# Layer 1's q and k of a head pair by seven products of quarters

## The chip, the cores and the metric

The kernel runs on one core of a Trainium2 chip. The metric is the device time of one launch in microseconds (us); the figure for a kernel is the median of its runs. Before the change it is 3814.2 us (three runs, 3813.44 to 3816.28). Everything is computed in 32-bit floats.

## The reference, cut to what matters

Two attention layers run one after the other on four images of 32 x 32 tokens with 768 channels, each behind a group norm and with a residual. Layer 1 is the one that changes:

```python
qkv = x @ w_qkv.T + b_qkv
q, k, v = (qkv[0], qkv[1], qkv[2])
q = layer_norm(dwconv3x3(q, w_pool_q), g_q, b_q)
k = layer_norm(dwconv3x3(k, w_pool_k), g_k, b_k)
v = layer_norm(dwconv3x3(v, w_pool_v), g_v, b_v)
attn = jnp.einsum('bqc,bkc->bqk', qf * scale, kf)
attn = attn + rel_h[:, :, :, :, None] + rel_w[:, :, :, None, :]   # after a reshape
o = softmax(attn) @ vf + q
x = x + o @ w_proj.T + b_proj
```

There are 12 heads of 64. The change touches only `x @ w_qkv.T` for q and k.

## The kernel before, in words

**Tiles.** The 1024 tokens of an image lie along the free axis in two halves of 512 (`HALF`), the 768 channels as six chunks of 128 partitions. Two heads make a **pair** (128 rows of q, k or v); a stage, which is one image in one layer, has six pairs. The stages run in the order (image 0, layer 0), (1, 0), (0, 1), (1, 1), then the same for images 2 and 3: 8 stages, 48 pairs, of which 24 are of layer 1.

**The clock of the program.** `attend(pair)` (L720) gives out 16 steps per pair. Steps 0, 4, 8 and 12 emit a block of four score tiles (L820 and L822, and four exponentials on ScalarE, L827); steps 2, 6, 10 and 14 emit the 16 matmuls of the weighted sum that eat them (L844). Between two `yield`s the main loop takes the pieces that `events` holds for that step. So, while pair A is attended, the pieces of the pairs behind it are emitted; TensorE, VectorE, ScalarE and GpSimd have a manual schedule, and the emission is the order of their queues. A pair's plan (L643) gives each piece a number r; the piece of pair i falls in step 16(i-1)+r. So r from 0 to 15 is "pair A+1 in step r of A", and r from -8 to -2 is "pair A+2 in step r+16 of A". SyncE, which issues the loads and stores of SBUF, is not in the manual schedule.

**A pair of layer 1, before the change.** q, k and v each take six chunk products per half: `padded` (L517) makes 12 calls of a 64-column matmul (`halves`, L128, L131) into one PSUM bank, and ScalarE then writes the half into a padded image with two instructions (L527). VectorE runs the nine taps of the convolution (`taps`, L531: L542 once, L544 eight times), centres (L559, L560), sums squares (L570, L571), normalises (L157 to L160, L582), and for v that last step writes `vt`, which the weighted sum reads. By steps of the attended pair A:

- pair A+1: step 2 and 4 v halves; 2 to 6 taps of k; 3 centre q; 6 and 7 squares and norm of q; 8 centre k; 8 to 11 taps of v; 9 transposes of q back (`back`, L586) and its copies; 10 and 11 positions, and squares of k; 12 norm of k and `split` (L624: L630 on VectorE, then 16 DMAs on GpSimd's queue that lay out the position bias); 13 centre v; 14 transposes of k back; 15 squares and norm of v.
- pair A+2: step 9 and 10 the two q halves (8 and 10 for some pairs), 12 and 14 the two k halves, 12 to 15 eight of the nine taps of q; the ninth comes in step 0 of the next pair.
- pair A itself: in steps 4 and 12 four VectorE instructions of `result` (L800 to L805); in steps 2 and 10 `restore_last`, which needs the one small PSUM bank.

**PSUM.** `bank()` hands out half-size banks from the two places b and c that the score tiles also use, in the order that `behind_scores` and `behind_av` give; the next user of a place waits until the last reader of its bank is done. `small_bank` is one bank of its own.

**Weights.** `uses` lists the weight loads in the order of their use; two buffers, and `used()` issues the load of the use after next.

**Quarters, as they exist before.** Layer 0 (pairs 2 and on, `sevens`, L391) and the projections (`project`, L858) already multiply a 2 x 2 arrangement of quarters by seven products instead of eight. There the weight sums are made once by `mix_weights` (L268) and kept in DRAM, and the token sums lie in SBUF (`mix_tokens`).

Of the kernel before, what the change touches and what calls it, by code (L numbers as in the profile page):

```python
# [17 lines left out]
P = 128  # L18
B = 4
S = 32  # L20
# [25 lines left out]
def two_layers(ctx: ExitStack, tc: tile.TileContext, keep, x_in, wqkv, wproj, rels, windows, vrow, small, const, onehot, picks, out):  # L46
# [122 lines left out]
    def rows(x):  # L169
# [6 lines left out]
    V_SUMS, PROJ_SUMS = NC, NC + NC // 2  # L176
    mixed = [
        dram.tile([P, N_SUMS, NC // 2, P], F32, tag=f"mixed{u}", name=f"mixed{u}")
        for u in range(PROJ_SUMS + 2 * (NC // 2))
    ]  # L180
    mixed_there = set()
# [14 lines left out]
    terms = [part(2 * T + 9 * HALF + i * HALF, HALF) for i in range(2)]  # L196
    counts = {"pad": 0, "y": 0, "c": 0, "v": 0}
# [5 lines left out]
    def in_sevens(i):  # L203

        return items[i][1] == 0 and i >= 2

# [11 lines left out]
    for i, (_, layer, hp) in enumerate(items):  # L218
        first = (i - 1) * 16 + shift(i)
        if in_sevens(i):  # L220
            uses += [(first, (i, 0, 0)), (first + 0.1, (i, 0, 1)), (first + 2, (i, 0, 2)), (first + 2.1, (i, 0, 3))]
            if hp % 2 == 0:
                uses += [(first + 8, (i, 2, 0)), (first + 8.1, (i, 2, 1)), (first + 10, (i, 2, 2)), (first + 10.1, (i, 2, 3))]
        else:
            uses += [(first + r, (i, s)) for s, r in enumerate((-8, -4, 2) if layer else (0, 4, 8))]
# [15 lines left out]
    def load_weights(n):  # L241

        if n >= len(uses):
            return
        i, s, *some = uses[n]
        _, layer, hp = items[i]
        w = wp.tile([P, NC, P], F32, tag="wqkv", name="wqkv_t")
        weights[uses[n]] = w
        if not some:
            nc.sync.dma_start(w, wqkv[layer, hp, :, s])  # L250
        elif some[0] == 0:
            (pa, sa), (pb, sb) = two(i, s)
            nc.sync.dma_start(w[:, :3, :], wqkv[0, pb, :, sb, 3:])
            nc.sync.dma_start(w[:, 3:, :], wqkv[0, pa, :, sa, :3])
        else:
            load_sums(w, hp if s == 0 else V_SUMS + hp // 2, some[0])
# [11 lines left out]
    def mix_weights(u):  # L268
# [4 lines left out]
        if u < PROJ_SUMS:  # L273
            (pa, sa), (pb, sb) = two(u, 0) if u < V_SUMS else two(2 * (u - V_SUMS), 2)
            nc.sync.dma_start(a, wqkv[0, pa, :, sa])
            nc.sync.dma_start(b, wqkv[0, pb, :, sb])
        else:
            layer, m = divmod(2 * (u - PROJ_SUMS), NC)
            for i, w in enumerate((a, b)):
                nc.sync.dma_start(w, wproj[layer, :, :, m + i, :].rearrange("h p q -> p h q"))  # L280
        yield
        a1, a2, b1, b2 = a[:, :3, :], a[:, 3:, :], b[:, :3, :], b[:, 3:, :]
        for n, to, x, y, op in (
# [11 lines left out]
    def mix_tokens(stage):  # L295
# [3 lines left out]
        for to, x, y, op in (  # L299
# [3 lines left out]
            nc.vector.tensor_tensor(to, x, y, op)  # L303
            yield
# [70 lines left out]
    class Pair:  # L375
# [11 lines left out]

        def make_vt(self):
            self.vt = work.tile([P, NKT, P], F32, tag="vt", name="vt")
# [111 lines left out]
        def put_k(self, ps, h, scale, bias):  # L501
            if self.k is None:
                self.k = work.tile([P, T], F32, tag="k", name="k")
# [13 lines left out]
        def padded(self, s, h):  # L517
# [3 lines left out]
            ps = self.product(s, h)  # L521
            ps = ps.rearrange("p (a c) -> p a c", a=S)

            for g, own, there in ((h, slice(0, S // 2), 1), (1 - h, slice(-1, None) if h == 0 else slice(0, 1), 0 if h == 0 else S // 2 + 1)):
# [4 lines left out]
                )  # L529

# [112 lines left out]
        def plan(self):  # L643
# [14 lines left out]
            if not self.layer:  # L658
# [18 lines left out]
            pieces = [  # L677
                (-8 if early_late else -7, lambda: self.padded(Q, 0)),
                (-6, lambda: self.padded(Q, 1)),
                (-4, lambda: self.padded(K, 0)),  # L680
                (-2, lambda: self.padded(K, 1)),
# [301 lines left out]
    def at(step, piece):  # L983
        events.setdefault(step, []).append(piece)
# [3 lines left out]
    for k in range(1, len(stages)):  # L988
# [3 lines left out]
        for r in range(12):  # L992
            at(first + 2 * n_steps + 2 + 3 * r, lambda norm=norm: next(norm, None))
# [11 lines left out]
    for u, call, step in (  # L1005
        (2, 0, 5), (7, 6, 11), (3, 13, 18), (4, 22, 29), (8, 31, 38), (5, 40, 47), (0, 49, 55), (6, 57, 63), (1, 65, 71),
        (9, 72, 77), (10, 78, 83), (11, 84, 89), (12, 124, 135), (13, 137, 147), (14, 149, 159),
# [358 lines left out]
```

## Time and profile before

The table is of the profiled execution, which took 3816.61 us by its own clock; its span, first to last instruction, is 3814.6 us. The median of the three timed runs is 3814.2.

| engine | busy us | share of the span |
|---|---|---|
| TensorE matmul (PE) | 3749.5 | 98% |
| VectorE (DVE) | 2467.1 | 65% |
| ScalarE (ACT) | 1786.5 | 47% |
| GpSimd (POOL) | 529.1 | 14% |

The granted TensorE clock is 0.997. DMA moved 330.44 MB, a mean of 87 GB/s. A pair of layer 0 takes some 55 to 75 us and a pair of layer 1 some 72 to 74 us between the first score matmuls of two attended pairs, longer where a projection runs beside it (up to 114 us). "PE busy" is pipelined matmul time, so the useful reading of it is how little is left idle. Idle time of another engine matters only where TensorE waits for it.

### The profile page before, as it was taken

The page shows a single profiled execution, that of the slowest core. Times are in us where ns is not written, and L with a number is a line of the kernel's source. Part 1 is how long each engine was busy: PE and PEld are TensorE (multiplying, and loading weights), DVE is VectorE, ACT ScalarE, POOL GpSimd, SP SyncE. Part 2 cuts the span into 40 slices and gives each one's busy share as a digit, 9 for nine tenths or more (in the row PEclk, how much of TensorE's full clock was granted, in tenths as well). Part 3 has the DMA queues.
Part 4 walks back from the last instruction along what each step waited for, and adds up shares of the span by engine and source line. Part 5 has one row for each costly group of instructions (what it writes and reads, how often), then busy time and mean ns, then how long its engine had stood idle before and what let it go on. Part 6 is the DMA issues. An engine that isn't in the chain of part 4 may idle for free. (4 is left out here: it accounts for less than half of the span.)

```text
span 3814.6 us, 76313 instructions
## 1 busy us (share of the span) xinstructions
PE 3749.5 (98%) x32990; PEld 1656.7 (43%) x32990; DVE 2467.1 (65%) x3068; ACT 1786.5 (47%) x2573; POOL 529.1 (14%) x964
## 2 busy tenths in 40 slices
PE   8999999999999999999999999999999999999998
PEld 4535535533344443444535445355343444434442
DVE  2566554559678877688454554445686888867874
ACT  2455434545355553455534544254442555525562
POOL 0111100111111211111200010001111112111120
PEclk9999999999999999999999999999999999999999
DMA  4344443331431223311333132523114212142123
GB/s 152 102 122 116 134 144 90 101 81 40 119 102 48 57 59 95 123 48 48 82 111 121 53 78 63 171 61 78 46 46 131 87 50 66 47 122 65 48 58 100
DMA packets 214024, 330.44 MB, mean 87 GB/s; under 512 B 50390, under 2 KB 103698, under 8 KB 213680
## 3 DMA queue, kind: packets, MB, share of 16 engines
q1 hardware_dynamic: 122912, 211.86, 17.9%
q0 software_dynamic: 90768, 113.61, 12.6%
q8 instruction: 263, 4.31, 0.5%
q14 instruction: 81, 0.66, 0.1%
HBM read 184.23 MB, written 40.10 MB: 59 GB/s over the span
## 5 line engine op out<-in xcount | busy, mean ns | idle before, releaser
L827 ACT ACTIVATE e<-s 128x1024 f32<-128x1024 f32 x768 | 775.6, 1024 | 423.7 <-PE s L822 393.6
L131 PE MATMUL qkv<-xn,wqkv_t 128*64 128x512 f32 x3648 | 816.0, 596 | 7.0 <-DVE gmean L334 2.6
L820 PE MATMUL s<-q,k 64*128 64x512 f32 x3072 | 808.7, 603 | 6.6 <-ACT e L827 3.1
L544 DVE SCALAR_TENSOR_TENSOR shared<-shared,sm 128x1056 f32<-128x1056 f32 x576 | 757.9, 1316 | 15.7
L822 PE MATMUL s<-bias,ones 64*128 64x512 f32 x1536 | 611.7, 790 | 1.1 <-DMA bias<-whole 1.0
L844 PE MATMUL av<-e,vt 128*64 128x512 f32 x2624 | 596.2, 596 | 0.0
L131 PEld LDWEIGHTS qkv<-xn,wqkv_t 128*64 128x64 f32 x3648 | 256.5, 137 | 484.0 <-issue 466.1
L640 POOL DMA_DIRECT2D bias<-high x384 | 205.6, 556 | 1794.6 <-ACT high L629 1559.7
L838 DVE TENSOR_TENSOR acc<-acc,e 128x1024 f32<-128x1024 f32 x294 | 360.0, 1225 | 114.0 <-ACT e L827 87.4
L820 PEld LDWEIGHTS s<-q,k 64*128 64x128 f32 x3072 | 279.5, 186 | 264.4 <-issue 213.3
L527 ACT ACTIVATE shared<-qkv,sm 128x512 f32<-128x512 f32 (+1 forms) x288 | 129.3, 502 | 469.7 <-PE qkv L131 469.7
L844 PEld LDWEIGHTS av<-e,vt 128*64 128x64 f32 x2624 | 185.4, 137 | 350.9 <-issue 316.8
L822 PEld LDWEIGHTS s<-bias,ones 64*128 64x128 f32 x1536 | 148.6, 187 | 185.4 <-issue 184.1
L640 POOL DMA_DIRECT2D bias<-whole x384 | 207.2, 571 | 53.2 <-DVE whole L630 46.3
L836 DVE TENSOR_TENSOR acc<-e 128x1024 f32<-128x1024 f32 x49 | 60.0, 1225 | 215.4 <-ACT e L827 206.8
L742 ACT COPY weighed<-av 128x512 f32<-128x512 f32 x96 | 56.3, 587 | 279.0 <-PE av L844 270.1
L559 DVE TENSOR_REDUCE mean<-ln_c 128x8 f32<-128x512 f32 x144 | 98.6, 685 | 106.0 <-PE ln_c L556 106.0
L771 POOL DMA_DIRECT2D weighed<-last x94 | 50.7, 541 | 679.6 <-ACT last L768 638.6
L613 PEld LDWEIGHTS rel<-q,rel 64*32 64x32 f32 x6144 | 112.1, 106 | 68.6 <-issue 63.8
L613 PE MATMUL rel<-q_t,rel 64*32 64x32 f32 x6144 | 123.6, 195 | 1.8 <-issue 1.8
L613 PE MATMUL rel<-q,rel 64*32 64x32 f32 x6144 | 122.7, 195 | 1.9 <-issue 1.9
L412 DVE TENSOR_TENSOR shared<-shared,m3m 128x512 f32<-128x512 f32 x66 | 45.3, 687 | 119.9 <-PE m3m L131 119.8
(162 smaller groups left out, 4439.0 us busy)
## 6 DMA issues: line engine op xcount, KB each, us to landing
bias<-high POOLq DMA_DIRECT2D x384, 128.0 KB, 2.9
bias<-whole POOLq DMA_DIRECT2D x384, 128.0 KB, 3.0
wqkv_t<-in_wqkv SPq DMA_DIRECT2D x78, 384.0 KB, 3.2
wqkv_t<-mixed SPq DMA_DIRECT2D x66, 384.0 KB, 3.1
wproj_t<-mixed SPq DMA_DIRECT2D x48, 384.0 KB, 3.3
wqkv_t<-in_wqkv SPq DMA_DIRECT2D x66, 192.0 KB, 2.5
xn<-in_x SPq DMA_DIRECT2D x24, 512.0 KB, 7.7
x<-in_x SPq DMA_DIRECT2D x48, 256.0 KB, 3.2
```

Source lines behind the costliest of these rows:

```text
L131: nc.tensor.matmul(ps[lo : lo + D], a[:, lo : lo + D], b, start=start, stop=stop, **kw)
L527: nc.scalar.activation(self.pad[s][:, rows, there : there + src.shape[2]], src, AF.Identity, bias=col(self.column(s)))
L544: nc.vector.scalar_tensor_tensor(y, window, tap, y, ALU.mult, ALU.add)
L559: nc.vector.tensor_reduce(of, heads, AX.X, ALU.add)
L613: nc.tensor.matmul(ps[lo : lo + S, k * S : (k + 1) * S].rearrange("p (b c) -> p b c", b=2), rel[rows, 2 * self.layer + i, first : first + ...
L640: nc.gpsimd.dma_start(sets, some.unsqueeze(1).to_broadcast([D // 2, 2, QC]))
L820: nc.tensor.matmul(ps[:, j, :], k[rows, keys], q[rows, cols], start=True, stop=False)
L822: nc.tensor.matmul(ps[:, j, :], ones[rows, kt % 2 * P : (kt % 2 + 1) * P], bias[c][rows, kt // 2, :], start=False, stop=True,)
L827: nc.scalar.activation(e, ps, AF.Exp)
L836: nc.vector.tensor_tensor(acc, es[0], es[1], ALU.add)
L838: nc.vector.tensor_tensor(acc, acc, e, ALU.add)
L844: nc.tensor.matmul(av[j * D : (j + 1) * D, :], pair.vt[:, kt, j * D : (j + 1) * D], e[:, j, :], start=(kt == 0), stop=(kt == NKT - 1),)
```

## The change

For 22 of the 24 pairs of layer 1 (all but the first pair after layer 0, twice), q and k of a pair are one product of a 2 x 2 arrangement: rows q and k, columns the two token halves, inner index the two groups of three channel chunks. It is done by seven products of three chunks each (`seven`, 6 matmul calls) in the form with few sums of results. Terms:

- `sum_tokens` makes four token sums per chunk column of a stage once, on VectorE (12 instructions of 128 x 512 per stage), and stores each in DRAM (`tokens`), in nine pieces from step 62 of the stage before. `call` loads one kind of sum (three blocks of 256 KB) from DRAM; each pair calls four kinds in turn into the same three blocks.
- `mix_weights` makes the weight sums of the six pairs once (24 VectorE instructions in all) while layer 0 runs, and stores them.
- `products(n)`: n=0 in step 6 of A (three products w1, w6, w2), n=1 put first in step 8 (w7), n=2 in step 9 (w4), n=3 in step 12 (w5), n=4 in step 14 (w3). They replace the four halves that stood in steps 9, 10, 12 and 14. One half still goes out through ScalarE (`put_from`); the three others by `put_padded` on VectorE (one instruction of 128 x 512 with a running sum, one copy of a column of 128 x 32). Three more VectorE additions of 128 x 512 make the running sums.
- The group norm of a layer-1 stage begins 7 steps earlier. `k` and `vt` change from two rotating buffers to named ones; layer 1 has one of each, and the spare ones hold the blocks and the running sums. The times of some weight mixes move.

The other pieces of the plan keep their steps. The diff, cut:

```diff
+    def in_products(i):
+
+        return items[i][1] == 1 and items[i - 1][1] == 1
...
+        elif in_products(i):
+            uses += [(first + r, (i, 0, n)) for n, r in enumerate((-10, -8, -7, -2))] + [(first + 2, (i, 2))]
...
+        if u >= LATE_SUMS:
+
+            t1, t2 = (
+                wp.tile([P, HALF], F32, tag="x", name="mix")[:, : 3 * P].rearrange("p (n c) -> p n c", c=P) for _ in range(2)
+            )
+            for n, to, x, y in ((3, t1, b1, a1), (0, t2, b2, t1), (1, b1, b2, b1), (2, a2, a2, t2)):
+                nc.vector.tensor_tensor(to, x, y, ALU.subtract)
+                nc.sync.dma_start(mixed[u][:, n], to)
...
+    def sum_tokens(stage):
+
+
+        for n in range(NC // 2):
+            x11, x12, x21, x22 = (xns[stage][:, n + k, h : h + HALF] for h in (0, HALF) for k in (0, 3))
+
+            def keep_sum(which, x, y, op):
+                to = wp.tile([P, HALF], F32, tag="x", name="token_sum")
+                nc.vector.tensor_tensor(to, x, y, op)
+                nc.sync.dma_start(tokens[stages.index(stage) % 2][which, n], to)
+                return to
...
         def make_vt(self):
-            self.vt = work.tile([P, NKT, P], F32, tag="vt", name="vt")
+            self.vt = one.tile([P, NKT, P], F32, tag=self.home("vt"), name="vt")
...
+        def call(self, which):
+
+
+            if which == S2:
+                two_blocks = one.tile([P, 2, HALF], F32, tag="vt0", name="blocks")
+                self.blocks = [two_blocks[:, 0], two_blocks[:, 1], third_block]
+            for n, block in enumerate(self.blocks):
+                nc.sync.dma_start(block, tokens[stages.index((self.b, self.layer)) % 2][which, n])
+
+        def seven(self, ps, at, x, more=False):
+
+            w = weights[self.i, 0, at // 2][:, 3 * (at % 2) : 3 * (at % 2) + 3, :]
+            for n in range(3):
+                halves(ps, w[:, n, :], x[n], start=not (n or more), stop=n == 2, skip_group_check=True)
+
+        def put_padded(self, s, h, ps, term):
...
+            nc.vector.scalar_tensor_tensor(own, as_image(ps), col(self.column(s)), as_image(term), ALU.add, ALU.add)
+            from_c, to_c = (S // 2 - 1, 0) if h == 0 else (0, S // 2 + 1)
+            rows = slice((1 - h) * (S + 2) + 1, (1 - h) * (S + 2) + 1 + S)
+            nc.vector.tensor_copy(pad[:, rows, to_c : to_c + 1], own[:, :, from_c : from_c + 1])
+
+        def products(self, n):
...
+            if n == 0:
+                self.call(S2)
...
+                self.seven(self.b1, 0, x[0, 0])
+                nc.scalar.copy(self.u, self.b1)
+                self.seven(self.b2, 2, self.blocks)
+                self.call(S3)
+                self.seven(self.b1, 1, x[0, 1], more=True)
+                used((self.i, 0, 0))
+                add(self.u, self.u, self.b2)
+                self.put_from(Q, 0, self.b1)
+            elif n == 1:
+                self.b1 = small_bank("w7w4")
+                self.seven(self.b1, 3, self.blocks)
+                self.call(S1)
+                used((self.i, 0, 1))
+                add(self.x, self.u, self.b1)
+            elif n == 2:
+                self.seven(self.b1, 4, x[1, 1], more=True)
+                self.put_padded(Q, 1, self.b1, self.u)
+            elif n == 3:
+                self.pad[K] = in_turn("pad", pads)
+                ps = bank("w5")
+                self.seven(ps, 5, self.blocks)
+                self.call(S4)
+                used((self.i, 0, 2))
+                self.put_padded(K, 1, ps, self.x)
+                add(self.u, self.u, ps)
+            else:
+                ps = bank("w3")
+                self.seven(ps, 6, self.blocks)
+                used((self.i, 0, 3))
+                self.put_padded(K, 0, ps, self.u)
...
+            if in_products(self.i):
+                pieces = [(r, lambda n=n: self.products(n)) for n, r in ((0, -10), (1, -8.5), (2, -7), (3, -4), (4, -2))]
...
     def at(step, piece):
-        events.setdefault(step, []).append(piece)
+
+        if step % 1:
+            events.setdefault(int(step + 0.5), []).insert(0, piece)
+        else:
+            events.setdefault(step, []).append(piece)
...
-            at(first + 2 * n_steps + 2 + 3 * r, lambda norm=norm: next(norm, None))
+            at(first + 2 * n_steps + (2 if stages[k][1] == 0 else -5) + 3 * r, lambda norm=norm: next(norm, None))
+        if stages[k][1]:
+            token_sums = sum_tokens(stages[k])
+            for r in range(9):
+                at(first + 4 * n_steps - 2 + r, lambda token_sums=token_sums: next(token_sums))
...
-        (9, 72, 77), (10, 78, 83), (11, 84, 89), (12, 124, 135), (13, 137, 147), (14, 149, 159),
+        (9, 72, 77), (10, 78, 83), (11, 84, 89), (16, 114, 119), (17, 120, 125), (18, 126, 131), (19, 132, 137),
+        (20, 138, 143), (15, 144, 149), (12, 150, 156), (13, 168, 174), (14, 176, 182),
```

## The prediction

> **What bounds the kernel now.** I read the page's engine shares first, then the groups, then one steady stretch of layer 1 by windows, then that stretch in order of time on VectorE and on TensorE. The page:
>
> ```profile
> PE 3749.5 (98%) x32990; PEld 1656.7 (43%) x32990; DVE 2467.1 (65%) x3068; ACT 1786.5 (47%) x2573; POOL 529.1 (14%) x964
> L131 PE MATMUL qkv<-xn,wqkv_t 128*64 128x512 f32 x3648 | 816.0, 596 | 7.0 <-DVE gmean L334 2.6
> L544 DVE SCALAR_TENSOR_TENSOR shared<-shared,sm 128x1056 f32<-128x1056 f32 x576 | 757.9, 1316 | 15.7
> ```
>
> TensorE is never idle for long (3814.6 - 3749.5 = 65 us in all), so work taken from it counts, if no other engine steps in. A chunk product (128 x 128 weights, 512 tokens) is 4 instructions: 816.0 us / (3648 / 4) = **0.895 us**. Now one attended pair of layer 1, without a projection or group norm (columns: us, then busy us and instructions of PE, PEld, DVE, ACT, POOL; clock; DMA), and its last two quarters (steps 8 to 15):
>
> ```profile
> 3230.60:3303.00 72.40, 72.40 (x610) 30.21 (x608) 57.31 (x70) 40.36 (x62) 14.01 (x25) 1.00 0.22 54
> 3258.60:3303.00 44.40, 44.40 (x470) 19.11 (x468) 36.14 (x45) 25.82 (x39) 12.16 (x22) 1.00 0.26 64
> ```
>
> VectorE is busy 57.3 of 72.4 us, but 36.1 of 44.4 in the second part: its slack is 8 us there. The order of time on VectorE in that part (start, length, then the idle time before):
>
> ```profile
> 3266.69 0.68 DVE L559 TENSOR_REDUCE mean<-ln_c 128x8 f32<-128x512 f32 x1
> ...
> 3270.13 8.09 DVE L544 SCALAR_TENSOR_TENSOR shared<-shared,sm 128x1056 f32<-128x1056 f32 x6
> ...
> 3284.22 0.75 DVE L805 SCALAR_TENSOR_TENSOR q<-inv,sm,q 128x512 f32<-128x512 f32 x1
> 3288.30 0.18 DVE L157 TENSOR_TENSOR t_ln<-r_ln 128x16 f32<-128x16 f32 x1 [3.33 <-ACT r_ln L155]
> ...
> 3296.10 5.37 DVE L544 SCALAR_TENSOR_TENSOR shared<-shared,sm 128x1056 f32<-128x1056 f32 x4
> 3304.38 0.17 DVE L157 TENSOR_TENSOR t_ln<-r_ln 128x16 f32<-128x16 f32 x1 [1.57 <-ACT r_ln L155]
> ...
> 3306.52 0.07 DVE L584 MEMSET vt<- 128x16 f32 x1
> ```
>
> From the centring of k (3266.69) to `vt` being complete (3306.6) VectorE has one unbroken list of 39.9 us, with only two idle spells, 3.33 and 1.57 us: **35.0 us of work**. While it idles for L157, taps whose images are ready stand behind: it does not take them early. The same part on TensorE:
>
> ```profile
> 3263.13 1.09 PE L556 MATMUL ln_c<-cst,shared 128*128 128x128 f32 x8
> 3264.15 5.37 PE L131 MATMUL qkv<-xn,wqkv_t 128*64 128x512 f32 x24
> ...
> 3286.78 5.37 PE L131 MATMUL qkv<-xn,wqkv_t 128*64 128x512 f32 x24
> 3292.09 1.09 PE L556 MATMUL ln_c<-cst,shared 128*128 128x128 f32 x8
> 3293.11 3.65 PE L844 MATMUL av<-e,vt 128*64 128x512 f32 x16
> 3296.69 1.09 PE L591 MATMUL ln_t<-cst,shared 128*128 128x128 f32 x8
> 3297.72 5.37 PE L131 MATMUL qkv<-xn,wqkv_t 128*64 128x512 f32 x24
> ```
>
> TensorE starts that part at 3263.1; the weighted sum that needs `vt` starts at 3307.6 (3303.0 plus the 4.55 that the score block takes): **44.4 us**, in which four halves of q and k (4 x 5.37 = 21.5) are the filler that gives VectorE its time. `vt` is ready 1 us before it is needed.
>
> [...]
>
> **The change part by part.**
>
> *TensorE, removed.* Per changed pair 24 chunk products become 21: 3 x 0.895 = 2.68 us. Over 22 pairs **59.0 us**. But they also move: three of the seven (8.05 us) go to step 6, where VectorE has slack, and w7 ahead of the centring in step 8. After w7, up to the weighted sum, TensorE now has 44.4 - 21.5 + 3 x 2.68 (w4, w5, w3) = **31.0 us** of work instead of 44.4.
>
> *VectorE, added.* The addition after w7 (0.69) stands ahead of the centring of k in the queue, so the list of 35.0 us can't start before w7 is done. In it come three `put_padded` and one more addition: 3 x (0.75 + 0.19) + 0.69. 0.75 is L918, a PSUM source of 128 x 512; its strided output is not in the trace, so 0.69 to 0.85. The copy of 128 x 32 has no row; the nearest is 0.175 at 128 x 16, so 0.1 to 0.3. List: 35.0 + 0.69 + 2.82 + 0.69 = **39.2 us**.
>
> *The new wait.* 39.2 against 31.0: TensorE waits at least 8.2 us per pair, first at the transposes of k (their bank is that of the centring of v, which VectorE reaches late; the before trace has this wait, ln_t for L560, at 6.1 us in all), then at the scores, since the exponentials stand on ScalarE behind the square root of v's norm, which waits for VectorE, then for `vt`. Idle spells of VectorE add to it: of the 3.33 I keep 1.0 (VectorE comes later, the four exponentials ahead of r_ln stay), of the 1.57 I keep 0.6 (the 0.9 of ScalarE's L527 goes), and 1.2 is new: w3's output is due behind the transposes of k (1.06 + 2.68 us of TensorE) while VectorE has only two taps (2.67). Together 2.8, bounds 0 and 3.33 + 1.57 + 1.2 = 6.1. So the wait is 11.0 us (8.2 to 14.3), and a pair gets 11.0 - 2.7 = **8.3 us longer** (5.5 to 11.6). The rest of the pair, 38.8 us of TensorE, has VectorE slack enough to start afresh each time.
>
> *Which pairs.* Products of pair i run while pair i-2 is attended. Sixteen of the 22 are like the one above: 16 x 8.3 = 133. In four, a projection runs in steps 9 to 15: it brings TensorE two rounds of 18.2 us and VectorE only some 20, so the count fits (59.7 against 67.4), but the two alternate; between -2.7 and +9, I take 5: 20. In two, the attended pair is of layer 0 and VectorE also adds up exponentials (L838, 7 x 1.225 = 8.6 in this part) against some 5 us more TensorE: -2.7 to +9, I take 6: 12.
>
> *Group norm and token sums.* Two of the four layer-1 stages are prepared while layer 1 is attended: 8 BATCH_NORM_STATS2 (5.4 us) move into steps 11 and 14, and 3 of the 12 token sums (2.1) into 14 and 15. 0 to 15 in all, I take 5. The rest lies in steps with slack or beside layer 0, where VectorE is busy 32 to 41 us of 55 to 75; so do the 24 weight sums (0.55 each). The token-sum stores (3.1 us landing) hold two buffers, at most a wait inside that slack: nothing.
>
> *DMA and SyncE's queue.* Per pair 12 block loads of 256 KB and two more weight loads. A `call` waits on SyncE for the product that read the blocks last; behind it is the weight load two uses on, which waits for that stage of products anyway. Landing of three blocks: 3.2 us (one block) to 8.2 (six of 512 KB, xn<-mid), say 5. S3 has w2 and a score block as cover, 7.0 us; S4 has 1.06 + 3.58 + 1.06 = 5.7, and 5 more where TensorE waits; S1 and S2 far more. So nothing; without cover, 2.5 us x 22 = 55.
>
> *ScalarE* loses three halves (3.0 us) and gains a copy (0.6). *Single `vt` and `k`:* `vt` is written from 3305.2, the sum that reads the old one ended at 3296.8; k's last scores are earlier still: nothing.
>
> Sum: 133 + 20 + 12 + 5 = **+170**. The profiled execution took 3816.6 (3814.6 of span, 2 around it), so 3987 for it; the median of the runs is 2.4 lower: **3984 us**.
>
> **The rivals.**
> *VectorE keeps up* (the other side): the price is then only the 59.0 us saved: 3755. Place: the list from w7 to `vt`. It decides at 31.0 + 2.7 = 33.7 us: below it the change gains. For it: VectorE's total is 57.3 + 4.9 = 62 of 69.8 us. Against: the order in the queue, and 35.0 us of rows already there.
> *VectorE keeps up, ScalarE does not:* from `restore_last`'s matmuls to the second copy of the positions ScalarE has 7.0 us (0.37, 2.36, 1.05, 3.2), and the third score tile waits for that bank with 4.7 us of TensorE before it, as the q half between is gone: 2.3 x 22 = 51, so 3806.
> *Blocks come late on top:* 3984 + 55 = 4039. For it: some 100 MB more on 330. Against: the engines are busy 31% now.
> That the products are not there: then 264 matmuls would not be missing (22 x 12).
>
> **How the numbers follow.** Likeliest case 0.80; late blocks on top 0.07; VectorE keeps up 0.07; ScalarE's wait alone 0.06. The likeliest's own range: low 16 x 5.5 - 6 x 2.7 = +72, 3886; high 16 x 11.6 + 6 x 9 + 15 = +255, 4069. Both slow cases hold 0.87; trimming a little above, 3880 to 4060 leaves 2 in 10 out. A measurement of this kernel tells about 0.2% (7.6 us) from no change. Faster: 0.07 and half of the 3806 case, 0.10; same 0.03; slower 0.87.
>
> **What would show it.** L131 qkv falls by 22 x 96 instructions and 22 x 84 come under new names. A steady attended pair takes some 81 us, with some 11 of PE idle, released by DVE L560 before ln_t and by ACT e before s; VectorE unbroken from w7's addition to L584. Wrong if PE idle in those pairs stays under 2.7 us, or if the releaser is a DMA of blocks.

## The result and the profile after

The changed kernel takes **4099.9 us** (median of four runs, 4090.9 to 4105.6) against 3814.7 us for the kernel before on the same chip: a ratio of **1.0745** (95% interval 1.0725 to 1.0766), 285 us more. Forecast were 3984 us and a range up to 4060. The direction was right; the rise of 170 us was 115 us too small. The profiled execution took 4098.3 us, with a span of 4096.4.

The engine shares of the kernel after, then the largest group of its products and another of as many matmuls (behind the bar: busy us and mean ns of one, then idle time ahead and what ended it):

```profile
PE 3803.5 (93%) x32726; PEld 1655.9 (40%) x32726; DVE 2607.3 (64%) x3338; ACT 1738.7 (42%) x2463; POOL 533.0 (13%) x964
...
L131 PE MATMUL w<-blocks,wqkv_t 128*64 128x512 f32 x528 | 151.8, 703 | 3.5 <-DMA wqkv_t<-mixed 2.0
...
L131 PE MATMUL w1w<-xn,wqkv_t 128*64 128x512 f32 x528 | 120.8, 592 | 0.0
```

TensorE has 32990 - 32726 = 264 instructions fewer, 22 x 12 as forecast. Yet it is *busy* for 54 us longer, and its idle time rose from 65 to 293 us. Work that should have taken 59 us less took 54 us more: 113 us of **stretch**, the time by which the same matmuls became slower. TensorE spent 246 us at half the full clock against 19 before, and half of these 227 us more is 113 us as well, so the sum agrees with the clock as its source. The second row holds over a quarter of it: 151.8 us where as many matmuls of the third row took 120.8, at 703 ns for one instead of 592.

What TensorE waited for in the kernel after (us in total, times, longest):

```profile
PE ln_t L719 <- DVE shared L688: 65.8, 18, 6.6
PE s L953 <- ACT e L960: 58.0, 21, 3.8
PE rel L741 <- issue: 47.0, 23, 2.5
PE p1p L131 <- DVE os_sums L1056: 24.1, 8, 5.8
PE ln_t L719 <- DVE shared L710: 18.2, 10, 4.7
```

The first two are the places that the prediction named: the transposes of k behind the centring of v (L688; 6.1 us before, as L560), and score tiles behind ScalarE's exponentials. The third was not in the likeliest case: the second half of the positions, with one wait in nearly every attended pair from 11 to 22 and 36 to 46. In the kernel before it had two:

```profile
PE rel L613 <- issue: 3.7, 2, 1.9
```

They stood in pairs 22 and 46, the two in which no q half of a layer-1 pair comes between the halves of the positions. So what went is its cover: work on TensorE beside which the wait did not show. What releases it isn't shown. In pair 41 it starts 0.23 us after ScalarE's first copy of the positions ends, but in other pairs anywhere from 1.5 us before that end to 2.0 us behind it. TensorE's waits for the DMA of blocks come to some 2.6 us in all.

Attended pair 41, the one that the prediction took apart (72.4 us before), by windows: the pair (3446.28 to 3531.67), and the section from the end of w7 to the weighted sum that needs `vt`:

```profile
3446.28:3531.67 85.39, 75.29 (x599) 31.40 (x597) 61.74 (x79) 38.36 (x57) 13.67 (x24) 0.94 0.32 90
3492.64:3539.48 46.84, 36.73 (x408) 16.79 (x409) 39.60 (x57) 21.27 (x31) 11.23 (x20) 0.89 0.44 119
```

In the pair TensorE is idle for 10.1 us and busy for 2.9 us more with 2.7 us less to do. In the section VectorE is busy for 39.6 us (forecast 39.2). TensorE is busy for 36.7 us where 31.0 were forecast, at a granted clock of 0.89.

The same section in order of time on VectorE, where it idled, and its ends:

```profile
3492.68 0.69 DVE L621 TENSOR_TENSOR temps<-temps,w7w 128x512 f32<-128x512 f32 x1 [9.10 <-PE w7w L131]
...
3517.32 0.17 DVE L157 TENSOR_TENSOR t_ln<-r_ln 128x16 f32<-128x16 f32 x1 [2.16 <-ACT r_ln L155]
...
3531.79 0.75 DVE L607 SCALAR_TENSOR_TENSOR shared<-w,sm,temps 128x512 f32<-128x512 f32 x1 [2.54 <-PE w L131]
...
3539.35 0.07 DVE L712 MEMSET vt<- 128x16 f32 x1
```

VectorE stands 9.10 us *before* w7's addition, the slack of the first part of the pair. Behind it the list is not unbroken: the two spells shown and two shorter ones (0.77 ahead of k's squares, 0.53 ahead of v's L157) make 6.0 us. And on TensorE:

```profile
3495.49 1.49 PE L719 MATMUL ln_t<-cst,shared 128*128 128x128 f32 x8 [1.82 <-DVE shared L710]
3496.91 4.01 PE L131 MATMUL w7w<-xn,wqkv_t 128*64 128x512 f32 x12
...
3526.82 1.09 PE L719 MATMUL ln_t<-cst,shared 128*128 128x128 f32 x4 [3.03 <-DVE shared L688]
...
3538.14 1.13 PE L953 MATMUL s<-q,k 64*128 64x512 f32 x4 [2.94 <-ACT e L960]
```

These are waits of 1.8 to 3.0 us, with slow matmuls behind the first: w4 (the row `w7w<-xn`) takes 4.01 us, where twelve such matmuls take 2.68.

The next table cuts pair 41 at four marks: its first score matmul, the first transpose of k for the centring (L556, later L684), VectorE's L157 of k's norm, and `vt` complete. C reaches 3.6 to 7.8 us into the next pair.

| kernel | A: start of pair to transposes of k | B: to L157 of k | C: to `vt` | pair |
|---|---|---|---|---|
| before | 32.6 | 25.2 | 18.3 | 72.5 |
| after | 46.3 | 24.8 | 22.1 | 85.4 |
| without VectorE's share (e8) | 44.0 | 21.2 | 17.6 | 76.4 |
| filler (e3) | 46.3 | 24.1 | 20.5 | 83.2 |
| v's taps early (e4) | 47.9 | 24.4 | 22.1 | 86.6 |
| q's taps late (e5) | 46.3 | 24.5 | 15.9 | 81.6 |

A grew by 13.7 us: four of the seven products moved into it (10.7), and it has the wait of 2.9 for the exponentials. Some 13.4 us of TensorE's work left B and C, but in this pair B is no shorter and C longer. Other pairs divide the loss between A and B in another way: in pairs 16 and 40 A is 50.3 and 50.4 us, B 22.1 and 20.4. A and B together took 57.8 to 57.9 us before in six steady pairs (14, 16, 17, 40, 41 and 44), and take 70.8 to 72.4 after, with only 2.7 us more of TensorE's work.

Means per attended pair over all pairs, in us (idle: TensorE; half: time at a granted clock of 0.5). "Sixteen" are the layer-1 pairs that the prediction called steady, "four" those with two rounds of a projection, "two" the layer-0 pairs, "last" the pairs 22 and 46, the second last of each row of twelve layer-1 pairs, with which no products run:

| kernel | sixteen: pair, idle, half | four | two | last | all idle | all half |
|---|---|---|---|---|---|---|
| before | 77.7, 0.5, 0.0 | 111.9 | 77.1 | 58.6 | 51 | 19 |
| after | 89.0, 9.8, 8.8 | 127.3 | 86.7 | 64.0 | 280 | 246 |
| e1 sums only | 78.0, 0.6, 0.4 | 112.0 | 77.8 | 57.7 | 59 | 26 |
| e3 filler | 87.7, 4.4, 2.0 | 129.5 | 86.0 | 60.8 | 158 | 106 |
| e8 without VectorE's share | 82.0, 5.3, 3.6 | 113.9 | 83.5 | 58.5 | 162 | 92 |
| e7 reordered | 81.0, 4.9, 2.6 | 123.8 | 79.7 | 67.1 | 182 | 122 |
| e10 reordered 2 | 79.7, 3.9, 1.9 | 124.2 | 80.6 | 63.1 | 161 | 112 |
| e11 the same without VectorE's share | 78.6, 2.8, 2.1 | 116.2 | 80.5 | 62.9 | 128 | 87 |
| e13 before, v's taps early | 84.8, 5.5, 5.8 | 121.3 | 83.0 | 64.7 | 177 | 171 |

Of the 285 us, 16 x 11.3 = 181 lie in the sixteen, 4 x 15.4 = 62 in the four, 2 x 9.6 = 19 in the two, 2 x 5.4 = 11 in the last, 9 in the other 24 and 3 outside of the pairs.

### The profile page after: what moved, and what is told of

Same layout as the page of the kernel before. It is cut to its first block, busy times and chain, and to the rows that moved or that the text cites. A ratio compares the mean times of both kernels' runs of the same rounds, so it can differ in the third digit from the quotient of the medians.

```text
span 4096.4 us, 76705 instructions
## 1 busy us (share of the span) xinstructions
PE 3803.5 (93%) x32726; PEld 1655.9 (40%) x32726; DVE 2607.3 (64%) x3338; ACT 1738.7 (42%) x2463; POOL 533.0 (13%) x964
## 5 line engine op out<-in xcount | busy, mean ns | idle before, releaser
L953 PE MATMUL s<-q,k 64*128 64x512 f32 x3072 | 834.0, 620 | 63.9 <-ACT e L960 58.0
L955 PE MATMUL s<-bias,ones 64*128 64x512 f32 x1536 | 627.5, 809 | 3.6 <-DMA bias<-high 2.4
L977 PE MATMUL av<-e,vt 128*64 128x512 f32 x2624 | 604.9, 604 | 0.1
L131 PE MATMUL qkv<-xn,wqkv_t 128*64 128x512 f32 x1536 | 341.7, 595 | 0.9 <-DVE xn L399 0.9
L768 POOL DMA_DIRECT2D bias<-whole x384 | 212.5, 578 | 56.5 <-DVE whole L758 47.9
L131 PEld LDWEIGHTS qkv<-xn,wqkv_t 128*64 128x64 f32 x1536 | 106.9, 137 | 209.9 <-issue 203.4
L131 PE MATMUL w<-blocks,wqkv_t 128*64 128x512 f32 x528 | 151.8, 703 | 3.5 <-DMA wqkv_t<-mixed 2.0
L741 PE MATMUL rel<-q_t,rel 64*32 64x32 f32 x6144 | 124.8, 196 | 20.4 <-issue 20.4
L583 ACT ACTIVATE shared<-qkv,sm 128x512 f32<-128x512 f32 x112 | 50.2, 502 | 215.7 <-PE qkv L131 215.7
```

Source lines behind the costliest of these rows:

```text
L131: nc.tensor.matmul(ps[lo : lo + D], a[:, lo : lo + D], b, start=start, stop=stop, **kw)
L741: nc.tensor.matmul(ps[lo : lo + S, k * S : (k + 1) * S].rearrange("p (b c) -> p b c", b=2), rel[rows, 2 * self.layer + i, first : first + ...
L768: nc.gpsimd.dma_start(sets, some.unsqueeze(1).to_broadcast([D // 2, 2, QC]))
L953: nc.tensor.matmul(ps[:, j, :], k[rows, keys], q[rows, cols], start=True, stop=False)
L955: nc.tensor.matmul(ps[:, j, :], ones[rows, kt % 2 * P : (kt % 2 + 1) * P], bias[c][rows, kt // 2, :], start=False, stop=True,)
L977: nc.tensor.matmul(av[j * D : (j + 1) * D, :], pair.vt[:, kt, j * D : (j + 1) * D], e[:, j, :], start=(kt == 0), stop=(kt == NKT - 1),)
```

## The experiments

The theories at the start: **the list** (the prediction's: VectorE's queue from w7 to `vt` is longer than TensorE's work beside it), **the clock** (the waits bring TensorE to half clock, 246 us of it in the trace, and the stretched matmuls are the loss), **the blocks** (DMA), **ScalarE** (rival 2's chain of copies) and **the preparation** of a stage. Each run's ratio is to the kernel before on the same chip.

**e1: the preparation alone.** No pair takes the products; sums and stores stay.

```diff
-        return items[i][1] == 1 and items[i - 1][1] == 1
+        return False
```

> The changed kernel with in_products always false: q and k of layer 1 are made as before, but the weight sums, the token sums with their stores, the earlier group norm and the single k and vt stay. If the excess of 285 us comes from the products' place in VectorE's queue (my theory): 3815 to 3830, the +5 (0 to 15) of the prediction. If the preparation per stage is what was under-priced: 3850 or more.

Measured: 3827.4 us, 1.0033 (1.0021 to 1.0044). Token sums, stores and group norm cost 12.0 us; forecast were 5, 0 to 15. The other 273 us are the products'.

**e2: the blocks.** The blocks are fetched once per pair.

```diff
+            if which != S2:
+                return
             for n, block in enumerate(self.blocks):
```

> The changed kernel with three of the four calls of token sums per pair left out (the products read the first kind four times, so their values are wrong): 9 of 12 block loads per pair and their waits go. Theory of VectorE's queue and of the clock: 4090 to 4105, no change. Theory of late blocks or of DMA load: lower by 40 us or more.

Measured: 4095.6 us, 1.0739 (1.0719 to 1.0759), within the interval of the change. Three quarters of the block traffic cost nothing; the rival of late blocks is out.

**e3: the clock.** Matmuls on constants fill three places where TensorE waits.

```diff
+            if followed(self.i) and s == 1 and h == 1:
+                fill(small_bank("fill"), 3)
             ps = bank("ln_t")
+            if followed(self.i) and s == 0 and h == 0:
+                fill(ps, 2)
...
+                    if kt == 3 and c == 0 and followed(pair.i):
+                        fill(small_bank("fill"), 3)
```

> The changed kernel plus 8 filler matmuls of 128x128 by 512 (0.9 us each, results unused) per changed pair, put where TensorE waits: two before the transposes of q, three between those of k, three before the fourth score tile of step 0. No wait is shortened by them. Theory that the waits let TensorE fall to half clock and that this costs time on the path: half-clock stretches go, 3990 to 4050. Theory that the stretched matmuls lie inside waits anyway: 4095 to 4120.

Measured: 4073.6 us, 1.0672 (1.0654 to 1.069), between the two expectations. Of the 246 us at half clock 140 vanished, some 59 of the 113 us of stretch went (TensorE is busy for 3902.5 us, of which 157.5 are filler), and the kernel gained 26. Its mean clock is 0.987, against 0.970 after and 0.997 before. A steady pair went from 89.0 to 87.7: 77.7 of before, less 2.7 saved, 3.9 more idle, 7.2 of filler (eight matmuls of 0.895) and 1.6 of stretch.

But not all of the filler stands in a wait. In the kernel after TensorE waited ahead of q's transposes for 8 of the 22 changed pairs only, between k's transposes for 18, and at the fourth score tile for 18. So some 47 us of filler were put where nothing was waited for, and the 26 us understate what the half clock costs. In the six steady pairs that waited at all three places (14, 17, 20, 38, 41 and 44) 4.0 us of stretch went per pair, and 2.6 us came back. In the four steady pairs with one round of a projection, which waited between k's transposes alone, 2.2 us of stretch went, and the pair still got 1.4 us longer. So the stretch costs time, but not all of it; how much over the whole kernel isn't settled.

**e4: the list.** The nine taps of v go to steps 6 to 8, six of them ahead of q's norm.

```diff
-                (V, 8, (2, 2, 3, 2)),
             )
+            pieces.insert(0, (7, lambda: self.taps(V, 2, 6)))
...
+            pieces += [(6, lambda: self.taps(V, 0, 2)), (8, lambda: self.taps(V, 6, 9))]
```

> The changed kernel with the nine v taps of a layer-1 pair in steps 6 (two), 7 (four, ahead of q's norm) and 8 (three) instead of 8 to 11: VectorE's idle time while TensorE makes w1, w6, w2 takes six of them, and the list between w7 and vt falls by 7.4 us to 31.8. VectorE's list with clock: the wait per pair falls from 11 to about 3.6 us and the half clock goes with it, 3830 to 3870. VectorE's list without the clock being on the path: 4100 less 22 x 7.4, about 3937. If VectorE's list is not what holds TensorE: 4090 to 4105.

Measured: 4092.6 us, 1.0719 (1.0701 to 1.0737). The list theory missed by over 150 us; the third expectation held. VectorE in pair 41 of this run:

```profile
3506.85 1.22 DVE L698 TENSOR_REDUCE lnv<-shared 128x16 f32<-128x1024 f32 x1 [5.49 <-ACT shared L694]
3515.52 0.18 DVE L157 TENSOR_TENSOR t_ln<-r_ln 128x16 f32<-128x16 f32 x1 [4.41 <-ACT r_ln L155]
```

What was taken from the list turned into idle time: 5.49 us ahead of the squares of k (0.77 before that edit) and 4.41 ahead of its norm (2.16). B is 24.4 against 24.8 us, C the same 22.1. Over the six steady pairs A and B together take 70.5 us on average, against 71.6. So VectorE does not run one list from w7 to `vt`. As the traces read, the end of B is set by TensorE and ScalarE in turn (transposes of q, w4, weighted sum, `last`, ScalarE's copies, positions, scores, four exponentials, r_ln), and only C is VectorE's. The new theory was: the *places* of w7's addition and of q's taps hold up this chain.

**e5 and e6: q's taps.** In e5 q's taps go three steps later, so that less stands on VectorE at the end of a pair. e6 adds e4's edit.

```diff
-                (Q, -4, (2, 2, 2, 2, 1)),
+                (Q, -1, (3, 3, 3)) if in_products(self.i) else (Q, -4, (2, 2, 2, 2, 1)),
```

> The changed kernel with the nine q taps of a changed pair behind the norm of v (three each in step 15 and in steps 0 and 1 of the next pair) instead of steps 12 to 15 and 0. New theory: the run of VectorE that holds TensorE begins anew in step 12, when ScalarE releases the norm of k after the four exponentials; from there to vt it has some 20 us of work against 15.4 of TensorE, and six or more taps (7.4 us) leave it: the waits before the transposes of k and before the fourth score tile go and the half clock behind them, some 5 to 9 us per pair, 3920 to 3990. The theory of the prediction (one list from w7 on) expects the same cut as for the v taps, 22 x 7.4, about 3937, but was refuted for those; if the wait is at some other engine: 4080 to 4105.

> The q taps late and the nine v taps early (steps 6, 7, 8) together. New theory: the v taps free VectorE before step 12 only, where ScalarE's release comes last anyway, so it is within 15 us of the run with q taps late alone. If both lists count: some 100 us lower than that run, near 3850.

Measured: 4033.0 us, 1.0576 (1.0558 to 1.0593), and 4024.3, 1.0549 (1.0531 to 1.0566). The two are close, as the new theory had it, and in pair 41 C falls to 15.9 us in e5, as it should where VectorE sets its end. The range given for e5 was too low. Its waits:

```profile
PE ln_c L684 <- DVE shared L672: 54.8, 20, 5.0
PE rel L741 <- issue: 47.5, 23, 2.6
PE ln_t L719 <- DVE shared L688: 28.9, 17, 4.3
```

The wait of the transposes of k fell from 65.8 to 28.9, and the one at the score tiles left the head of the list. In their place TensorE waits 54.8 us for q's own taps, now late. The positions' wait did not move.

**e7: the products reordered.** v's taps go early as in e4, and q's two steps later (steps 14, 15, 0 and 1). w7 comes not before q's transposes but between the two positions (step 10), and w4 behind the second (step 11). VectorE's share of w5 comes one step behind its matmuls, and w3 one step later (step 15).

```diff
-                pieces = [(r, lambda n=n: self.products(n)) for n, r in ((0, -10), (1, -8.5), (2, -7), (3, -4), (4, -2))]
+                pieces = [(r, lambda n=n: self.products(n)) for n, r in ((0, -10), (1, -6), (2, -5), (3, -4), (5, -3), (4, -1))]
...
+            elif n == 5:
+                self.put_padded(K, 1, self.b5, self.x)
+                add(self.u, self.u, self.b5)
```

> Both tap moves, and the products in other steps: w7 in step 10 and w4 in step 11, each behind one of the two positions pieces (so ScalarE's chain of square and copies gets TensorE work beside it), w5's two uses on VectorE behind the centring of v, w3 in step 15 behind the norm of v; q taps in steps 14, 15, 0 and 1. New theory: no hand-over from VectorE is late by more than 2 us, so of the 59 us saved some 20 to 45 are left after the 12 us of preparation: 3785 to 3830. If the array's half clock or another wait stays: 3850 or more.

Measured: 3944.3 us, 1.0343 (1.0326 to 1.0361): over half of the loss is gone, but another wait stayed, as the second expectation had it. The positions' wait did go in all pairs in which 2.7 us of w7 now stand between (47.0 to 4.4 us, the last line here; the two that are left are pairs 22 and 46). New ones came:

```profile
PE ln_t L720 <- DVE shared L711: 60.2, 19, 6.9
PE ln_c L685 <- DVE shared L673: 27.4, 16, 6.3
...
PE rel L742 <- issue: 4.4, 2, 2.5
```

```profile
ACT inv L919 <- DMA t<-z: 102.4, 16, 9.4
```

TensorE's transposes of q now wait for q's norm (L711): w7 no longer stands ahead of them, and on VectorE v's early taps stand ahead of the norm. ScalarE stands up to 9.4 us for `t<-z`, a transfer that GpSimd issues behind the 16 bias transfers of the pair.

**e8: without VectorE's share.** The seven products stay; VectorE's additions do not.

```diff
-                add(self.x, self.u, self.b1)
...
-                self.put_padded(Q, 1, self.b1, self.u)
+                self.put_from(Q, 1, self.b1)
...
-                self.put_padded(K, 1, ps, self.x)
-                add(self.u, self.u, ps)
+                self.put_from(K, 1, ps)
...
-                self.put_padded(K, 0, ps, self.u)
+                self.put_from(K, 0, ps)
```

> The seven products of each pair stand where the change put them, but what VectorE does with them is left out: w7's addition, the last addition to u, and the three halves written by VectorE; ScalarE writes those halves from the banks instead, as it does in the kernel before (so q and k of these pairs lack terms). TensorE's work and order are those of the change; VectorE's are those of the kernel before, but for one addition. It separates the two halves of the prediction's comparison 39.2 against 31.0: the loss of cover on TensorE (44.4 to 31.0), and the 4.2 us more on VectorE. If the loss of cover is enough by itself, the list of 35.0 still exceeds 31.0 by 4.0, idle spells of some 2.8 come on top, and the half clock stretches matmuls: some +4 to +6 us per steady pair over the kernel before, 3890 to 3960. If the added work and its place ahead of the centring are the cause, TensorE hardly waits and the 59 us saved show: 3770 to 3810.

Measured: 3913.5 us, 1.0262 (1.0245 to 1.0279), in the range of "the loss of cover is enough by itself". A steady pair is 4.3 us longer than before, with an idle time of 5.3. What is left of the waits:

```profile
PE rel L739 <- issue: 45.3, 22, 2.4
PE ln_t L717 <- DVE shared L686: 44.4, 18, 5.2
```

So in this order, of the 285 us, 99 stay without VectorE's share (12 of them the preparation), though TensorE's 59 are saved, and 186 come with that share. The positions' wait hardly changes (45.3 against 47.0), so VectorE's additions are not its cause. In the four pairs beside a projection nearly all is VectorE's: 113.9 without it, 127.3 with it. In pair 41, B is 3.6 us shorter than after; no addition of w7 stands ahead of q's norm there, and q's second half is no longer VectorE's.

**e10 and e11: both waits of e7 mended, with and without VectorE's share.** `sums` of a pair's second half comes two steps later, and two of v's taps go behind q's norm (the cut shows e10 against e7).

```diff
+                    later = c == 1 and pair.i + 2 < len(items) and in_products(pair.i + 1) and in_products(pair.i + 2)
-                    n_parts = 2 if short(pair.i) and (pair.hp, c) in ((NC - 2, 1), (NC - 1, 0)) else 1
+                    n_parts = 2 if later or short(pair.i) and (pair.hp, c) in ((NC - 2, 1), (NC - 1, 0)) else 1
...
-            pieces.insert(0, (7, lambda: self.taps(V, 2, 6)))
+            pieces.insert(0, (7, lambda: self.taps(V, 2, 4)))
...
-            pieces += [(6, lambda: self.taps(V, 0, 2)), (8, lambda: self.taps(V, 6, 9))]
+            pieces += [(6, lambda: self.taps(V, 0, 2)), (7, lambda: self.taps(V, 4, 6)), (8, lambda: self.taps(V, 6, 9))]
```

> The reordered kernel with the two waits mended that its trace shows in a steady pair: the sums of a pair's second half of queries are called two steps later (step 4 instead of 2), so that ScalarE no longer stands 9.4 us for t<-z with v's half behind it; and of the four taps of v ahead of q's norm in step 7, two go behind it, so that the norm comes 2.7 us sooner. If those waits are what is left, a steady pair falls from 81.0 to 75 to 77 us and the kernel to 3840 to 3890. If VectorE is simply full there, the waits move to the next place: 3920 to 3960.

> The order of the second reordered kernel, and VectorE's share of the products left out as in the run without it (w7's addition, the last addition to u; three halves of q and k are written by ScalarE from the banks, so q and k of these pairs lack terms). If the loss of cover on TensorE is a matter of order alone, the 59 us that the seven products save now show, less the 12 us of the group norm and token sums: 3770 to 3810, below the kernel before. If no order gives back the cover that the halves of q and k were, the wait stays as without VectorE's share in the first order: 3850 to 3915. Against 3920 with VectorE's share, the difference is the price of its additions in a mended order.

Measured: 3920.1 us, 1.0276 (1.0259 to 1.0294): the second expectation, the waits move on. And 3869.9 us, 1.0145 (1.0128 to 1.0162): even with VectorE's additions for nothing, this order does not give the cover back, as its second expectation had it. The price of the additions is 50 us here.

**e12: some pairs.** The four pairs prepared beside a projection go back to their halves.

```diff
-        return items[i][1] == 1 and items[i - 1][1] == 1
+        return items[i][1] == 1 and items[i - 1][1] == 1 and i not in (14, 20, 38, 44)
```

> The second reordered kernel, with the products taken back for the four pairs that are prepared while a projection runs (pairs 14, 20, 38 and 44; they get q and k by the four halves). Those attended pairs took 124.2 us against 111.9 before: if the loss is theirs alone, 3920 less 4 x 12.3, 3865 to 3880. If part of it moves to their neighbours, whose rows they delayed, 3885 to 3910. It stays above the kernel before either way, as a steady pair there takes 79.7 against 77.7.

Measured: 3937.6 us, 1.0322 (1.0305 to 1.034). Both ranges failed: it is slower than e10, and the four attended pairs take 127.0 us *without* products. So another edit that they carry is enough to lengthen them; v's early taps are the candidate.

**e13: the control.** The kernel before with e4's edit and nothing else.

> A control: the kernel before, without the products, with nothing but v's taps moved forward as in the run with v's taps early (two in step 6, four ahead of q's norm in step 7, three in step 8). If moving taps costs nothing by itself, it stays at 3814 within 6 us and the four pairs beside a projection at 112. If the move is what kept those four pairs at 127 when their products were taken away, they take 122 to 128 here too and the kernel is at 3850 to 3885.

Measured: 3989.4 us, 1.0461 (1.0443 to 1.0478): **moving nine taps forward, with no work added, costs 175 us** in the kernel before, more than either expectation had. Its waits, and the place in pair 40, on TensorE and on VectorE:

```profile
PE ln_t L591 <- DVE shared L582: 134.0, 24, 8.0
```

```profile
3325.09 1.94 PE L591 MATMUL ln_t<-cst,shared 128*128 128x128 f32 x8 [6.31 <-DVE shared L582]
```

```profile
3317.60 5.38 DVE L544 SCALAR_TENSOR_TENSOR shared<-shared,sm 128x1056 f32<-128x1056 f32 x4
...
3323.72 1.22 DVE L582 TENSOR_TENSOR shared<-shared,r_ln 128x1024 f32<-128x1024 f32 x1
```

Four taps (5.38 us) stand ahead of q's norm on VectorE, and TensorE's transposes of q wait 6.31 us for it. This fits the theory of places, and qualifies e4, e6, e7 and e10, which carry the same move. The four pairs beside a projection take 121.3 us here against 111.9, so the early taps alone explain 9.4 of the 15.1 that e12 left there. In e4's pair 41 itself q's transposes waited 1.83 us (1.82 after), so its reading of B and C stands.

**e14 and e15: e10's order with v's taps back in their place**, with and without VectorE's share (the cut shows e14 against e10).

```diff
-            pieces.insert(0, (7, lambda: self.taps(V, 2, 4)))
-            pieces += [(6, lambda: self.taps(V, 0, 2)), (7, lambda: self.taps(V, 4, 6)), (8, lambda: self.taps(V, 6, 9))]
+                (V, 8, (2, 2, 3, 2)),
```

> The second reordered kernel with v's taps back where the kernel before has them (steps 8 to 11), so that q's norm has no taps of v ahead of it. The control says the early taps cost some 7 us per steady pair by themselves, by the wait of the transposes of q for q's norm. If that wait was what was left in the reordered kernels, this one falls from 3920 to 3820 to 3880, and the pairs beside a projection from 124 to about 115. If the early taps paid for themselves by shortening the list from w7 to vt, the waits come back at the transposes of k and the score tiles: 3920 or more.

> The same without VectorE's share of the products (w7's addition, the last addition to u, the three halves; q and k of these pairs lack terms). If order alone gives the cover back, the 59 us saved show at last: 3760 to 3815. If the loss of the halves' cover can't be mended by order, 3840 to 3900. The difference to the run with VectorE's share is the price of its additions in this order; the prediction's sum would have it at 4.2 us per pair where the list binds, some 90 us in all, and at nothing where it doesn't.

Measured: 3961.8 us, 1.0388 (1.0371 to 1.0405), and 3859.9, 1.0113 (1.0097 to 1.013). Both times the expectation with the longer time held, but e14's waits are not at the places that it named (transposes of k and score tiles). With VectorE's share the early taps pay for themselves (3920 with them), without it they bring nothing (3870 with them, and the two intervals touch). VectorE's share costs 102 us in this order (forecast for where the list binds: some 90). e14's waits:

```profile
PE ln_c L685 <- DVE shared L673: 34.4, 16, 6.7
PE w7w L131 <- DVE temps L621: 33.3, 17, 3.1
PE ln_t L720 <- DVE shared L711: 26.0, 8, 5.1
```

Three different places, all behind VectorE, none above 35 us: in each order tried, TensorE came to wait for another row of VectorE. That no order would do is not shown.

No version was faster than the kernel before. In e10 the four of the sixteen pairs with one round of a projection (18 us of other TensorE work) do show the saving: pairs 13, 19, 37 and 43 take 88.4 to 90.0 us against 91.2 to 92.8, which is 2.7 saved. By an estimate from these times, products for these four alone could bring some 11 us, against the 12 us of the preparation; it wasn't tried.

## Why the prediction was wrong

**Right: the direction and its ground.** Four halves of q and k were the filler under VectorE's rows; taken away, TensorE waited. 264 instructions and 59 us of TensorE's work went, the waits stand at the two named places, and the blocks cost nothing (e2): two of 256 KB landed in 3.0 us, the third in 4.6 (medians; `x<-in_x` of the same size took 3.2 before, the figure that the forecast used).

**Right in size: VectorE's rows, and the wait.** 39.2 us were forecast for the list, 39.6 are in the window. The plain additions took 0.68 to 0.69 us, the strided addition from PSUM 0.74 to 0.75, the small copy 0.20. The wait was forecast at 11.0 us per steady pair (8.2 to 14.3); TensorE's idle time is 10.1 us in the window of pair 41 (46.84 - 36.73), and rose by 9.3 us over the sixteen.

**The step that failed: TensorE's own time.** "TensorE now has 44.4 - 21.5 + 3 x 2.68 (w4, w5, w3) = 31.0 us of work" took for granted that the work runs at the speed of before while waits open beside it; the stretch was put at nothing. It took 36.7 us. A steady pair got 9.3 us of idle time and 4.7 of stretch, less the 2.7 saved, so 11.3 longer; the forecast had 11.0 of wait and no stretch, less 2.7, so 8.3. Over the kernel the forecast waits were 170 + 59 = 229 us and measured idle time rose by 228, so the 115 us that are missing are about the 113 of stretch. That the waits came out so well is luck in part: they were smaller than forecast in the sixteen (9.3 against 11.0) and larger in the four (12.1 against 7.7). And it is a sum, not yet the whole cause: e3's six pairs, where 2.6 of 4.0 us came back, suggest that a part of the stretch lies in time that would have been waited for anyway.

**A second wrong term: VectorE's idle spells, 2.8 us.** In pair 41 they are 6.0 us, near the upper bound given (6.1). L157 kept 2.16, not 1.0; w3's output cost 2.54, not 1.2 (0.97 with filler; of the 1.57 between, 1.10 are the slower product, 3.90 against 2.80 us, as the last section shows); 0.77 was not foreseen. The section from w7 to the weighted sum was forecast at 39.2 + 2.8 = 42.0 and took 46.8.

**Wrong step behind it: "one unbroken list".** B and C have different ends. e4 took work off B's list and B stayed at 24.4 us in pair 41; e5 took work off C's, and C fell from 22.1 to 15.9. The rows of before may have looked like one list because VectorE was nearly as long there as the chain through TensorE and ScalarE beside it; this was not tested. The rival on ScalarE was right in its ground, that the q half is gone from between the positions: 47.0 us stand there, a step earlier than placed, near its price of "2.3 x 22 = 51". That ScalarE's copies are what TensorE waits for isn't shown. The price was added nowhere, since the rivals were taken as exclusive.

**Wrong sizes elsewhere.** The four pairs beside projections: +5 forecast, +15.4 measured, of which 13.4 go with VectorE's share (e8). "The count fits (59.7 against 67.4)" is a count of busy time; but the projection's products then wait longer for the projection's additions (p1p for L1056: 24.1 us, before 7.4, and 7.7 in e8). That is 4 x 10.4 = 42 of the 115 us; the sixteen make 48, the two 7, the last pairs 11 (forecast at nothing), and all the rest, forecast as the 5 of preparation, 7. The upper bounds were per pair 11.6 and 9; the mean of the sixteen came to the first, and the four went over the second.

**Open.** How much of the 113 us of stretch costs time isn't settled: the filler of e3 also takes time on TensorE's queue, stood outside of a wait in places, and left 2.0 us of half clock per steady pair. Of e12's four pairs 5.7 us are unexplained, and so are the 5.4 us of pairs 22 and 46, in which no products run but rows of the pairs prepared with them do. What releases the positions isn't known, and ScalarE's chain of copies was not tested by itself.

## What to carry to other kernels

Work on the bounding engine can be the cover of a chain through the others: before removing it, cut the steady section at the points where the chain changes engine, and ask of each piece whether it would get shorter. A piece whose end is set by another engine need not get shorter when its work is moved out, while the work is paid for where it lands (here 10.7 us went into A, 13.4 us left B and C, and A and B together grew by 13 to 15 us). Price the work that stays at the speed that it will have beside the new waits (here w4 took 4.01 us behind one, not 2.68). And test an order by itself in the old kernel: nine taps moved forward looked harmless in the new one and cost 175 us in the old.

## What the runs showed of the hardware

In pair 41 TensorE's granted clock was 0.5 after waits of 1.82, 2.31 and 3.03 us. In the trace of the changed kernel it is 0.5 in 55 spans, 38 of them of 3.413 us and 15 of twice that, 246 us in all against 19 before; all 55 begin on one grid of 3.413 us. In pair 41 three such spans begin within 0.7 us of the ends of those waits. Two windows of that pair, each around the twelve matmuls of one product, w5 and w3 (the first number behind the times is the length, the third from the end the granted clock):

```profile
3515.80:3518.60 2.80, 2.80 (x15) 0.84 (x14) 1.14 (x5) 2.32 (x5) 0.08 (x1) 1.00 0.23 41
3527.84:3531.74 3.90, 3.90 (x15) 1.12 (x14) 1.38 (x2) 1.73 (x2) 1.04 (x2) 0.71 0.66 143
```

Without a wait ahead the product takes 2.80 us, behind the wait of 3.03 it takes 3.90. The length of a wait alone does not decide this: of the sixteen waits of 2.93 to 2.95 us at the fourth score tile, nine had a span at half clock at their end (running, or begun within 1 us), and seven had none, among them the one shown above (2.94). What the half clock costs in the end is less sure: 140 us of it less brought 26 us in e3, with some 47 us of filler outside of waits.
